# Counts of edges beside the keys, and x + b0 a step earlier, in a graph layer kernel

## The chip, the cores and the metric

The kernel runs on one core of one Trainium2 chip. The metric is the device time of one execution in microseconds (us). Before the change three runs took 4014.95, 4014.03 and 4009.7 us, median 4014.03. A core has five engines that the text speaks of by their names or by those of the profile: TensorE (PE, its weight loads PEld), VectorE (DVE), ScalarE (ACT), GpSimd (POOL) and SyncE (SP), which starts the transfers. Each works through its own instructions in order, and waits for the others by semaphores.

## The reference

There are 32 independent graphs of 512 nodes with 128 features. About one entry in 16 of an adjacency matrix is not zero.

```
# layer 0: normalised graph convolution, added to x, layernorm
adj1 = adj + I;  dinv = adj1.sum(axis=2) ** -0.5
x = layernorm(x + dinv[:,:,None] * adj1 * dinv[:,None,:] @ (x @ weight) + bias)
# layer 1: a message for every pair of nodes, weighted by adj, summed
m_j = x @ W1[:D];  m_i = x @ W1[D:]
msg = gelu(layernorm(m_j[:, None] + m_i[:, :, None] + b1, g1, be1))   # pair (i, j)
agg = einsum('bijo,bij->bio', msg, adj)
x = layernorm(x + layernorm(concat([x, agg]) @ W2 + b2, g2, be2))
```

## The kernel before, in words

A message is needed only where adj is not zero, so the kernel lists the neighbours of every node and works through lists. For a batch (one graph) it makes `key`, which is the variance term of the message at edges and 0 elsewhere; VectorE's top-8 operations find the edges from it in slots of eight (`lists`), then up to 16 more (`more`), which are shared out over two further slots (`shared`). A batch is 41 groups: 8 slots of 4 groups, one group of own edges, and 2 slots of 4.

A group runs through a pipeline, one group behind the other (`pairs`, `sums`, `weights`, `messages`, `aggregate`): TensorE gathers the features of the neighbours by matmuls with one-hot matrices into one of three PSUM buffers `u` (L724, L725); VectorE adds to it and leaves `u_sb` (L734), which frees the buffer; GpSimd multiplies adjacency values with the one-hot matrix, the weight product `sw` (L749, four buffers); ScalarE makes four Gelus `m` (L763); TensorE sums with `agg` (L772). At the end of a batch ScalarE copies agg (L781), and `finish` does the last layernorms of that batch during the next one: on VectorE the statistics (L194, L196), on GpSimd rstd and shift (L199 to L205) and three products (L645, L647, L649), on ScalarE the scaling (L208).

Beside the groups of one batch the kernel prepares the next ones. Each preparation is a Python generator that is advanced a few steps per group; a table `plan` says in which groups: `layer0` of the next batch has 26 steps over the first 22 groups of the current batch, `more` and `shared` of the current batch run from group -10 to 28. For ScalarE, GpSimd and VectorE the instructions stand in the order in which the program writes them in this loop; TensorE and SyncE are ordered by a planner. What comes before the loop, batch 0's preparation among it, is ordered by the planner on all engines.

The steps of `layer0` that matter here, in order: transposes of the adjacency into `a_t`, and on ScalarE a pass over each quarter that sums the degrees (`copied`, L260); on VectorE `mask`, -1 at edges and 0 elsewhere, in bf16 (L263); two pauses; on GpSimd the degree chain deg1, none, degp, rdeg, dinv, dinv2 (L277 to L287) and `xb` = x + b0 (L289); on ScalarE four passes over the mask that count the edges (L293), then `s` and `own_s`, the features scaled by dinv (L297, L302), from the PSUM tile psup; two steps later GpSimd adds own_s to xb (L306) and TensorE makes `pconv` in two halves of eight matmuls (L311); VectorE makes y (L318), its statistics follow, GpSimd's rstd and shift, ScalarE's x1 (L208), TensorE's transposes (L220), and so on to the keys: in five steps (L358) TensorE makes pv (L365) and VectorE reads it a step later, twice for each quarter (L361, L362). The counts of edges are read by GpSimd much later, in `shared` (L499), to see that no edge was missed.

`shared` runs at the same time as these last steps, with the shared slots of the current batch: L469 to L479 on VectorE right after `more` ends; then 16 pairs of matmuls `pl` on TensorE (L537), each copied by ScalarE into `sent` (L533), and `chosen` on VectorE (L553), which reads all of `sent` and lies in the same buffer as the mask. The PSUM tiles outside the pipeline come from a pool of four banks.

Of the kernel before, what the change touches and what calls it, by code (L numbers as in the profile page):

```python
# [8 lines left out]
F32 = mybir.dt.float32  # L9
BF16 = mybir.dt.bfloat16  # L10
I32 = mybir.dt.int32
U32 = mybir.dt.uint32
AF = mybir.ActivationFunctionType
ALU = mybir.AluOpType
# [4 lines left out]
P = 128  # L19
# [8 lines left out]
def bcast(ap, n):  # L28

    return ap.unsqueeze(1).to_broadcast([ap.shape[0], n, ap.shape[-1]])  # L30
# [16 lines left out]
def sparse_path(ctx, tc, x, adj, w0, b0, w1, b1, g1, be1, w2, b2, g2, be2, out, most):  # L47
# [21 lines left out]
    nc = tc.nc  # L69
    B, N, D = x.shape  # L70
    C = N // P
# [3 lines left out]
    node = ctx.enter_context(tc.tile_pool(name="node", bufs=1))  # L75
    small = ctx.enter_context(tc.tile_pool(name="small", bufs=2))
# [66 lines left out]
    rows = {}  # L143
# [69 lines left out]
    def bank(key):  # L213
        return ps.tile([P, 512], F32, tag="ps", name=key)
# [10 lines left out]
    def pause(n):  # L225

        for _ in range(n):
            yield

    def layer0(b):  # L230

        st = state[b] = {}
        xs = node.tile([P, C, D], F32, tag="xs", name=f"xs_{b}")
# [7 lines left out]
        edges = small.tile([P, C], F32, tag="edges", name=f"edges_{b}")  # L241
        st["edges"] = edges
        deg = small.tile([P, C], F32, tag="deg", name=f"deg_{b}")
        mask = big.tile([P, C, N], BF16, tag="mask", name=f"mask_{b}")
        px = transposed(xs, f"x_{b}")
        for mc in range(C):
# [12 lines left out]
            copied = small.tile([P, N], BF16, tag="copied", name=f"copied_{b}_{mc}", bufs=1)  # L259
# [11 lines left out]
            if mc == 0:  # L271
                x_t = node.tile([P, N], F32, tag="t0", name=f"x_t_{b}")
                nc.scalar.copy(x_t, px)
        yield from pause(2)

        deg1 = small.tile([P, C], F32, tag="deg1", name=f"deg1_{b}")
        nc.gpsimd.tensor_scalar(deg1, deg, 1.0, None, ALU.add)  # L277
# [7 lines left out]
        nc.gpsimd.tensor_sub(dinv, rdeg, none)  # L285
        dinv2 = small.tile([P, C], F32, tag="dinv2", name=f"dinv2_{b}", bufs=1)
        nc.gpsimd.tensor_tensor(dinv2, dinv, dinv, ALU.mult)  # L287
        xb = node.tile([P, C, D], F32, tag="t2", name=f"xb_{b}")
        nc.gpsimd.tensor_tensor(xb, xs, bcast(rows["b0"], C), ALU.add)  # L289

        for q in range(C):
            copied = small.tile([P, N], BF16, tag="copied", name=f"counted_{b}_{q}", bufs=1)
            nc.scalar.activation(copied, mask[:, q, :], AF.Copy, accum_out=edges[:, q : q + 1])  # L293

        s = node.tile([P, C, D], F32, tag="t1", name=f"s_{b}")
        for c in range(C):
# [60 lines left out]
        key = big.tile([P, C, N], F32, tag="key", name=f"key_{b}")  # L357
        for q in range(C + 1):  # L358
            if q:
                here = key[:, q - 1, :]  # L360
                nc.vector.scalar_tensor_tensor(here, pt, a_sum[:, q - 1 : q], c_sum, ALU.add, ALU.add)  # L361
                nc.vector.scalar_tensor_tensor(here, here, -TINY, mask[:, q - 1, :], ALU.min, ALU.mult)  # L362
            if q < C:
                pt = bank(f"pv_{b}_{q}")
                nc.tensor.matmul(pt, at2[:, q * P : (q + 1) * P], ct, start=True, stop=True)  # L365
            yield
# [417 lines left out]
    def advance(gens, steps=1):  # L784
# [13 lines left out]
    n_groups = len(order)  # L798
    plan = [
        (layer0, 26, -n_groups, -19),  # L800
        (lists, 21, -19, -8),
        (parts, 7, -19, -10),
# [343 lines left out]
```

## Time and profile before

| | |
|---|---|
| runs, median (lowest to highest) | 4014.03 us (4009.7 to 4014.95) |
| the profiled execution's own time | 4011.64 us |
| its span, first to last instruction | 4009.9 us |
| mean granted TensorE clock | 0.985 |
| TensorE matmuls / weight loads busy | 3766.3 us (94%) / 3510.3 us (88%) |
| VectorE, ScalarE, GpSimd busy | 3263.9 us (81%), 2791.9 us (70%), 2225.5 us (55%) |
| the four counts of a batch (L293), passes alone | 128 passes, 80.1 us, mean 626 ns |
| xb (L289) | 32 times, 40.7 us, mean 1273 ns |
| the mask (L263) | 32 times, 39.0 us, mean 1218 ns |
| s / own_s (L297, L302) | 128 each, 361 ns / 394 ns |

The profile records one execution, instruction by instruction. A row of the timeline has the start in us from the first instruction, the duration, the engine, the line of the program, the operation, what it writes and reads, and how many alike follow each other (x4); in brackets the idle time of the engine ahead of it, and what ended it. A row of the list of waits has the waiting instruction, what it waited for, the time in total, how often, and the longest. A row of a table by stretches has the stretch, its length, the busy time of the five engines with the number of instructions, the granted clock (1.00 is full), the share of the DMA engines and GB/s. Busy time alone says little: an engine that works all the time may only be the one that all wait behind, and a wait matters only where nothing later takes its place.

### The profile page before, as it was taken

How to read it: one execution, taken by the hardware profiler on the slowest of the kernel's cores; microseconds unless marked ns; L12 is line 12 of the kernel's file. 1: busy time of each engine (PE TensorE's matmuls, PEld its weight loads, DVE VectorE, ACT ScalarE, POOL GpSimd, SP SyncE). 2: the span in 40 equal slices, each digit the busy share in tenths (PEclk: the TensorE clock that was granted, in tenths of full speed). 3: DMA queues.
4: the chain of work that ended last, by engine and by line, in shares of the span. 5: the costliest groups of instructions: out<-in, count | busy, mean ns of one | idle time of the engine just before them, and what ended most of it. 6: DMA issues, size and time to landing. Idle time of an engine off the chain costs nothing. (4 is left out here: it accounts for less than half of the span.)

```text
span 4009.9 us, 108439 instructions
## 1 busy us (share of the span) xinstructions
PE 3766.3 (94%) x39744; PEld 3510.3 (88%) x39744; DVE 3263.9 (81%) x10645; ACT 2791.9 (70%) x8321; POOL 2225.5 (55%) x2526
## 2 busy tenths in 40 slices
PE   5999999999999999999999999999999999999997
PEld 5988889888899888898888998888998889888887
DVE  6888888888887888888888888888888888788892
ACT  4777677676776766776767767667767677676664
POOL 4555565555655555655556555556555565555554
PEclk7999999999999999999999999999999999999998
DMA  3444444444444444444444444444444444444442
GB/s 85 107 109 106 114 101 106 107 107 105 113 102 106 108 106 110 106 106 106 107 105 113 102 106 108 106 112 104 106 105 108 105 108 106 108 107 105 98 105 56
DMA packets 902107, 419.99 MB, mean 105 GB/s; under 512 B 724304, under 2 KB 882192, under 8 KB 901568
## 3 DMA queue, kind: packets, MB, share of 16 engines
q1 hardware_dynamic: 901344, 412.52, 44.1%
q8 instruction: 317, 5.19, 0.5%
q14 instruction: 222, 1.82, 0.1%
q0 software_dynamic: 224, 0.46, 0.1%
HBM read 227.15 MB, written 13.76 MB: 60 GB/s over the span
## 5 line engine op out<-in xcount | busy, mean ns | idle before, releaser
L749 POOL TENSOR_TENSOR sw<-mt,a_t 128x512 f32<-128x512 bf16 x1056 | 1216.8, 1164 | 918.1 <-PE agg L772 764.0
L772 PE MATMUL agg<-sw,m 128*128 128x128 f32 x10496 | 1495.7, 285 | 76.2 <-POOL sw L749 46.1
L724 PE MATMUL u<-c,s 128*128 128x128 bf16 x15744 | 1433.9, 220 | 84.0 <-DVE u_sb L734 80.3
L763 ACT ACTIVATE m<-u_sb,r 128x128 f32<-128x128 f32 x4096 | 1294.0, 395 | 142.3 <-DVE u_sb L734 57.8
L772 PEld LDWEIGHTS agg<-sw,m 128*128 128x128 f32 x10496 | 1304.5, 192 | 94.2 <-POOL sw L749 51.3
L724 PEld LDWEIGHTS <-s 128*128 128x128 bf16 x15744 | 1191.2, 98 | 115.0 <-issue 40.9
L725 PE MATMUL u<-be,sd_rows 128*128 128x128 bf16 x5248 | 1148.6, 220 | 20.7 <-DMA sd_rows<-sd_ds 14.6
L734 DVE TENSOR_TENSOR u_sb<-u,ac 128x512 f32<-128x512 f32 x1056 | 713.4, 676 | 200.6 <-PE u L725 177.1
L725 PEld LDWEIGHTS <-sd_rows 128*128 128x128 bf16 x5248 | 512.7, 98 | 30.7 <-issue 20.0
L763 ACT ACTIVATE m<-u,r_s 128x128 f32<-128x128 f32 x1024 | 288.3, 363 | 251.6 <-PE agg L772 247.4
L533 ACT COPY sent<-pl 128x352 f32<-128x352 f32 x512 | 228.9, 447 | 315.9 <-PE pl L537 278.8
L687 DVE TENSOR_SCALAR s<-raw,node_p 128x2052 bf16<-128x2052 bf16 (+1 forms) x352 | 421.5, 1197 | 20.6 <-DMA raw<-idx_ds 11.9
L720 PE MATMUL u<-ac,sj 128*128 128x128 f32 x2048 | 437.8, 296 | 0.0
L749 POOL TENSOR_TENSOR sw<-mt,sent 128x512 f32<-128x512 bf16 x256 | 296.4, 1163 | 229.0 <-PE agg L772 176.2
L537 PEld LDWEIGHTS pl<-a_t,sj 128*128 128x128 f32 x2048 | 316.2, 191 | 60.7 <-issue 59.2
L457 DVE MAX8 a_t<-key 128x8 f32<-128x128 f32 x1024 | 301.2, 294 | 34.5
L537 PE MATMUL pl<-a_t,sj 128*128 128x176 f32 x2048 | 327.4, 313 | 1.3 <-POOL a_t L505 1.3
L522 DVE TENSOR_SCALAR sj<-pj,node_p 128x512 f32<-128x512 f32 x256 | 187.7, 745 | 153.8 <-PE pj L526 153.8
L720 PEld LDWEIGHTS u<-ac,sj 128*128 128x128 f32 x2048 | 310.0, 192 | 0.4
L458 DVE FIND_INDEX8 idx_m<-a_t,key 128x8 uint32<-128x128 f32 x1024 | 291.4, 285 | 0.0
L311 PEld LDWEIGHTS pconv<-s,a_t 128*128 128x128 f32 x1024 | 141.3, 214 | 57.1 <-ACT s L297 55.4
L361 DVE SCALAR_TENSOR_TENSOR key<-pv,a_sum,c_sum 128x512 f32<-128x512 f32 x128 | 95.7, 748 | 108.3 <-PE pv L365 108.3
(178 smaller groups left out, 4788.8 us busy)
## 6 DMA issues: line engine op xcount, KB each, us to landing
raw<-idx_d SPq DMA_DIRECT2D x256, 513.0 KB
raw<-idx_ds SPq DMA_DIRECT2D x64, 513.0 KB
a_nat<-in_adj_dram SPq DMA_DIRECT2D x32, 1024.0 KB
sd_rows<-sd_d SPq DMA_DIRECT2D x768, 12.0 KB
xs<-in_x_dram SPq DMA_DIRECT2D x32, 256.0 KB
out_dram<-o_sb SPq DMA_DIRECT2D x32, 256.0 KB
mt<-s SPq DMA_TRANSPOSE x352
raw<-idx_ds SPq DMA_DIRECT2D x32, 129.0 KB
```

What stands on the lines that cost most here:

```text
L457: nc.vector.max(found, k)
L458: nc.vector.max_index(idx[:, n, h : h + 8], found, k)
L533: nc.scalar.copy(sent[:, n - 1], pt[:, : SHARED * WIDE].rearrange("p (k w) -> p k w", w=WIDE))
L537: nc.tensor.matmul(pt[:, k * WIDE : (k + 1) * WIDE], sj[:, n, k * P : (k + 1) * P], at[:, n, :], start=True, stop=True,)
L687: nc.vector.tensor_scalar(s.rearrange("p (k e) -> p k e", k=3), raw, node_p, None, ALU.is_equal)
L720: nc.tensor.matmul(pu[:, c, :], place, state[b]["ac"][:, q, 0, :], start=first, stop=False)
L724: nc.tensor.matmul(pu[:, c, :], here, c3[:, k, c, :], start=(first and k == 0), stop=False)
L725: nc.tensor.matmul(pu[:, c, :], dev[:, q, c, :], be9, start=False, stop=(c == C - 1))
L734: nc.vector.tensor_tensor(u, pu, a if t == EXTRA else bcast(a[:, q, :], C), ALU.add)
L749: nc.gpsimd.tensor_tensor(sw, mt[:, 0] if t == EXTRA else mt[:, :, q, :], a, ALU.mult)
L763: nc.scalar.activation(m[:, c, :], u[:, c, :], AF.Gelu, scale=r[:, k : k + 1])
L772: nc.tensor.matmul(st["agg"][:, c, :], m[:, c, :], sw[:, c, :], start=(begin and c == 0), stop=(end and c == C - 1),)
```

## The change

Three edits in `layer0`. `xb` is made in the second of the two paused steps, so one step ahead of the degree chain, instead of behind it. The four counting passes are taken out of the step that makes `s`. Each of them is put into one of the four steps of the keys in which VectorE reads a quarter, ahead of that reading.

```
@@ layer0
-        yield from pause(2)
+        yield
+        xb = node.tile([P, C, D], F32, tag="t2", name=f"xb_{b}")
+        nc.gpsimd.tensor_tensor(xb, xs, bcast(rows["b0"], C), ALU.add)
+        yield
 
         deg1 = small.tile([P, C], F32, tag="deg1", name=f"deg1_{b}")
         nc.gpsimd.tensor_scalar(deg1, deg, 1.0, None, ALU.add)
@@
         nc.gpsimd.tensor_tensor(dinv2, dinv, dinv, ALU.mult)
-        xb = node.tile([P, C, D], F32, tag="t2", name=f"xb_{b}")
-        nc.gpsimd.tensor_tensor(xb, xs, bcast(rows["b0"], C), ALU.add)
-
-        for q in range(C):
-            copied = small.tile([P, N], BF16, tag="copied", name=f"counted_{b}_{q}", bufs=1)
-            nc.scalar.activation(copied, mask[:, q, :], AF.Copy, accum_out=edges[:, q : q + 1])
 
         s = node.tile([P, C, D], F32, tag="t1", name=f"s_{b}")
@@ the keys
         for q in range(C + 1):
             if q:
+
+                copied = small.tile([P, N], BF16, tag="copied", name=f"counted_{b}_{q}", bufs=1)
+                nc.scalar.activation(copied, mask[:, q - 1, :], AF.Copy, accum_out=edges[:, q - 1 : q])
                 here = key[:, q - 1, :]
                 nc.vector.scalar_tensor_tensor(here, pt, a_sum[:, q - 1 : q], c_sum, ALU.add, ALU.add)
```

In the changed program's order of instructions, VectorE and SyncE are as before. On GpSimd each xb stands seven places earlier: behind the shift of the layernorm in `finish` (L205), ahead of one weight product and of deg1. On ScalarE the four counts stand, in the loop, each behind the Gelus of one of the groups that carry `sent` copies: behind the first copy and before the second, before the sixth, before the twelfth, and before the last. In batch 0 they stand where they stood. On TensorE only the place of pconv's first half changes: it stood among the matmuls of the u of slot 2's second group, and the agg behind it was spread among them too; now two of its matmuls, two of the agg, one, two and five follow each other ahead of that u.

## The prediction

> **What bounds the kernel now.** I read the page's busy shares first, then the list of waits, then the timeline of one batch, and last the same stretch in all batches.
>
> ```profile
> PE 3766.3 (94%) x39744; PEld 3510.3 (88%) x39744; DVE 3263.9 (81%) x10645; ACT 2791.9 (70%) x8321; POOL 2225.5 (55%) x2526
> ```
> ```profile
> PE u L724 <- DVE u_sb L734: 80.3, 69, 2.2
> PEld pconv L311 <- ACT s L297: 55.4, 31, 6.7
> PE agg L772 <- POOL sw L749: 46.1, 30, 1.6
> PE agg L772 <- ACT m L763: 30.0, 20, 1.5
> ```
>
> TensorE is busy for 94%, but its few gaps lie at fixed places of each batch. The second wait line is the one that the change seems made for: once a batch pconv waits for `s`, which stands behind ScalarE's four counts. Whether that gap is worth anything depends on what ends later. I take the batch whose copy of agg (L781) starts at 1907.70; its period is 122.21 us. The timeline of all engines, columns start and duration in us:
>
> ```profile
> 1916.51 1.17 POOL L749 TENSOR_TENSOR sw<-mt,a_t 128x512 f32<-128x512 bf16 x1
> ...
> 1917.64 0.23 POOL L277 TENSOR_SCALAR deg<-deg 128x4 f32<-128x4 f32 x1
> ...
> 1918.14 1.22 DVE L263 TENSOR_SCALAR mask<-a_t 128x2048 bf16<-128x2048 f32 x1
> ...
> 1918.27 1.15 POOL L281 TENSOR_TENSOR degp<-deg,none 128x4 f32<-128x4 f32 x1
> ...
> 1920.98 0.61 ACT L293 ACTIVATE counted<-mask 128x512 bf16<-128x512 bf16 x1
> ...
> 1921.05 1.27 POOL L289 TENSOR_TENSOR xb<-xs,b_row 128x512 f32<-128x512 f32 x1
> ```
> ```profile
> 1925.75 1.27 POOL L647 TENSOR_TENSOR un<-un,be_row 128x512 f32<-128x512 f32 x1
> ...
> 1925.96 1.33 DVE L469 SCALAR_TENSOR_TENSOR over<-a_t,sharing 128x256 f32<-128x256 f32 x1
> ...
> 1926.98 1.45 POOL L306 TENSOR_TENSOR xb<-xb,own_s 128x512 f32<-128x512 f32 x1
> ```
> ```profile
> 1943.69 1.16 PE L772 MATMUL agg<-sw,m 128*128 128x128 f32 x8 [1.54 <-POOL sw L749]
> ```
>
> GpSimd works without a gap from 1914.59 to 1931.9, VectorE from 1910.2 on. VectorE reaches y (L318) at 1933.01 without having waited, its mean and variance go to GpSimd at 1935.25, GpSimd is again without a gap until the four weight products at 1942.47, and TensorE stands 1.54 us for the first of them. So in this third of the batch the chain GpSimd and VectorE, layernorm, GpSimd sets the time, not TensorE. The program shows it twice over, since some batches run the first half of pconv at half the clock. Two batches, 559.77 and 2029.91, TensorE's timeline, and their window of four us each (PEclk is the third number from the end):
>
> ```profile
> 581.50 1.95 PE L311 MATMUL pconv<-s,a_t 128*128 128x128 f32 x16
> ...
> 591.41 1.27 PE L772 MATMUL agg<-sw,m 128*128 128x128 f32 x8 [1.52 <-ACT m L763]
> ```
> ```profile
> 2053.27 1.95 PE L311 MATMUL pconv<-s,a_t 128*128 128x128 f32 x16
> ...
> 2061.60 1.27 PE L772 MATMUL agg<-sw,m 128*128 128x128 f32 x8
> ```
> ```profile
> 576.60:580.60 4.00, 3.99 (x41) 3.91 (x40) 3.89 (x8) 4.00 (x16) 4.00 (x5) 1.00 0.10 28
> ...
> 2046.70:2050.70 4.00, 3.96 (x22) 3.82 (x22) 3.90 (x8) 4.00 (x15) 4.00 (x5) 0.57 0.06 18
> ```
>
> Counted from each batch's copy, TensorE begins the second half of pconv at 21.73 in one and at 23.36 in the other, 1.63 us apart; y stands at 25.33 and 25.34 and that agg at 31.64 and 31.69. TensorE being 1.63 us earlier bought nothing.
>
> **The change part by part**, per batch, 31 batches in the loop.
>
> Counts out of the step of `s`: 4 x 0.75 us from start to start leave ScalarE; the first stood at 1920.98, `s` at 1923.86. Now `s` waits for dinv only. With xb in front, GpSimd ends dinv at about 1922.02 (below), so `s` comes some 1.8 us earlier. The new order on TensorE also places pconv's first half, with the agg of one group between, ahead of the whole next u instead of among it. This closes part of the 1.50 us gap that TensorE has before 1924.52 (that row names u_sb, ending at 1924.47; pconv's load waited 1.62 until then). Kept to the end: 1.50 x 31 = 46 us. By the two batches above, kept: 0; the time reappears at 1939.33 and 1943.69.
>
> Counts beside the keys: each stands behind a group's four Gelus and ahead of the `sent` copies. A copy that follows such a pass starts 0.61 to 0.63 after it. Three of the four meet a wait of ScalarE for pl of 1.93 us (1960.91, 1966.00, 1972.28) and vanish. The fourth does not:
>
> ```profile
> 1973.82 1.28 ACT L763 ACTIVATE m<-u_sb,r 128x128 f32<-128x128 f32 x4
> 1975.00 0.43 ACT L533 COPY sent<-pl 128x352 f32<-128x352 f32 x1
> ...
> 1976.24 1.23 DVE L553 SCALAR_TENSOR_TENSOR chosen<-sent,place_k 128x256 f32<-128x256 f32 x1
> ```
>
> That last copy moves to 1975.62 and ends at 1976.05. `chosen` reads all of `sent`, and its buffer is the mask's, so it also waits for the fourth count, a new wait, over by 1975.81. VectorE gets there at 1976.24: 0.19 us to spare, 0. Behind `chosen` VectorE is busy up to the indices for idx_h, for which TensorE waits in most batches, so without that cover it is 0.62 x 31 = 19 us. The Gelus behind move 0.62; their agg is 1.8 us after the first of them. The banks of the moved copies are wanted over 0.6 us later.
>
> xb: GpSimd's order puts it seven places up, ahead of one weight product and the degrees. 1.23 from start to start leave one place and enter another: 0 on GpSimd's own sum. The weight product moved back is read by TensorE after 1924: hidden. But the mask now meets something else. In the trace the mask holds up degp (1.15 instead of its shortest 0.20), and L469 cannot start before L647 (1.33 instead of 0.43). The Trainium skill, page "SBUF — State Buffer", section "Who interferes with whom", has the rule: a VectorE operation in a two-port mode, or with two SBUF inputs, and a GpSimd operation exclude each other for a whole instruction, first come first served. That speaks against this change: the weight product will run 1917.74 to 1918.91, and the mask, due at 1918.14, meets it. A blocked operation here ends as if begun 0.16 before the GpSimd end (L469: 1927.29 - 0.43 = 1926.86 against 1927.02), so the mask runs 1918.75 to 1919.97, 0.61 late. By the rule alone that is 0.61 x 31 = 19 us on VectorE. By the row it is 0: VectorE comes 0.61 later to L469, at 1926.57, and that waits for L647 until 1926.83 in any case. And GpSimd: deg1 ends 0.06 after the mask (as degp did), 1920.03; none, degp and rdeg start 0.08, 0.39 and 0.67 later; dinv is done at 1922.02, the next weight product starts at 1922.25 against 1922.28. It loses to the mask what it lost before. I take 0, bounds -0.1 and +0.1 a batch, 3 us either way.
>
> Half clock: it follows gaps of 0.84 and 1.50 us within 3.4 us. The page "TensorE: Matmul & The Clock Gate", part 1, halves the clock after an idle window of about 3.4 us; here 2.34 us of gaps were enough, so the row decides. After the change I count 1.45 (the next u waits for u_sb, 0.61 later) and 0.4 for the Gelus before the agg: 1.85. By the page, no half clock: 1.4 us saved in the one batch where y waited (0.92, at 2914) and 0.05 in ten others, -2 us. If it stays in 11 batches, y comes 0.3 late: +3. I take -1.
>
> Start: the first batch is ordered outside the written order; there the counts still stand ahead of `s`. 0.
>
> Sum: 0 + 0 + 0 - 1 = -1 on the profiled execution's 4011.64, of which the span is 4009.9; the runs' median is 2.4 above it. So about 4013.
>
> **The rivals.**
> TensorE keeps its gap: 4014 - 46 = 3968. For it: pconv <- s 55.4 us. Against: the two batches.
> The lock costs GpSimd less: were the mask not held by the weight product, degp's lost 0.95 would shrink and rdeg start 0.64 earlier; 0.64 x 31 = 20, 3994. Against: L479 (0.83 for four elements) ends with the weight product beside it.
> Slower by the lock: L469 has 0.26 us of room. If VectorE is later than about 0.87, L306 takes the ports first and L469, with the layernorm behind it, waits 1.23 more: 38 us, 4052. For it: only that margin.
> Slower by the fourth count: 0.2 to 0.62 a batch if `chosen` is ready sooner or ScalarE later: 4020 to 4033.
>
> **How the numbers follow.** Absorbed 0.66 (own range 4007 to 4020); gap kept 0.08; lock cheaper 0.08; lock lost 0.08; fourth count shows 0.10. 0.2% is 8 us, about what the runs can tell from no change. Faster 0.16, same 0.66, slower 0.18. The range leaves out the gap kept and the lock lost: 3993 to 4033.
>
> **What would show it.** `s` near 14.4 us after the copy of agg instead of 16.16; the mask at 1.8 us instead of 1.22, degp at 0.20; L469 still ending near 19.6; y near 25.3; the wait of agg for sw still about 1.5 or more; `chosen` at 68.5. It is wrong if y or `chosen` moves by more than 0.3 us in most batches.

## The result, and the profile after

| kernel | median | lowest to highest | runs |
|---|---|---|---|
| before, on the same chip | 4012.14 us | 4008.56 to 4016.68 | 12 |
| after | 4012.22 us | 4007.93 to 4016.84 | 12 |

The ratio is 0.9998, with a 95% interval of 0.9991 to 1.0006: no difference that can be measured. The forecast was 4013. The profiled execution of after took 4011.93 us, its mean granted clock is 0.985, as before. Its page:

```profile
span 4010.2 us, 108407 instructions
...
PE 3759.7 (94%) x39744; PEld 3502.1 (87%) x39744; DVE 3262.1 (81%) x10645; ACT 2785.8 (69%) x8321; POOL 2226.4 (56%) x2526
```

The total hides that the inside of a batch did change. The waits of after (us in total, times, longest):

```profile
ACT sent L533 <- PE pl L537: 221.4, 126, 3.1
...
PE agg L772 <- ACT m L763: 64.3, 31, 2.1
...
PE u L724 <- DVE u_sb L734: 54.5, 40, 2.2
...
ACT s L294 <- POOL dinv L288: 32.5, 31, 1.3
...
PE agg L772 <- POOL sw L749: 27.7, 22, 1.5
```

The wait of pconv for `s`, 55.4 us before, is gone from the list, and ScalarE now waits for dinv instead. TensorE's wait for u_sb fell by 25.8 us (from 80.3), and its wait for the Gelus `m` rose by 34.3 (from 30.0). That is the picture of time that moves, not of time that is gained. ScalarE's wait for pl fell by 57.4 us: the counts now lie in it.

The same batch as in the prediction, in after's timeline; its copy of agg starts at 1909.96:

```profile
1920.01 1.17 POOL L749 TENSOR_TENSOR sw<-mt,a_t 128x512 f32<-128x512 bf16 x1
...
1920.41 1.85 DVE L263 TENSOR_SCALAR mask<-a_t 128x2048 bf16<-128x2048 f32 x1
...
1921.14 1.20 POOL L280 TENSOR_SCALAR deg<-deg 128x4 f32<-128x4 f32 x1
...
1922.74 0.20 POOL L284 TENSOR_TENSOR degp<-deg,none 128x4 f32<-128x4 f32 x1
...
1924.37 1.14 ACT L294 ACTIVATE s<-psup,dinv 128x128 f32<-128x128 f32 x4 [1.03 <-POOL dinv L288]
...
1928.04 1.27 POOL L647 TENSOR_TENSOR un<-un,be_row 128x512 f32<-128x512 f32 x1
...
1928.86 0.74 DVE L469 SCALAR_TENSOR_TENSOR over<-a_t,sharing 128x256 f32<-128x256 f32 x1
...
1929.27 1.45 POOL L303 TENSOR_TENSOR xb<-xb,own_s 128x512 f32<-128x512 f32 x1
...
1935.31 1.08 DVE L315 SCALAR_TENSOR_TENSOR y<-pconv,dinv,xb 128x128 f32<-128x128 f32 x4
```

The mask is held by the weight product (1.85 us instead of 1.22), it holds up deg1 (1.20 instead of 0.23), and degp no longer loses anything (0.20 instead of 1.15). `s` starts 14.41 us after the copy instead of 16.16. L469 starts 0.6 us later than before and still ends at 19.64 (19.59 before), because it had waited for L647 before and now hardly does. y stands at 25.35 against 25.31. Over the 30 full batches the median of y moved from 25.33 to 25.37, that of `chosen` from 68.55 to 68.59.

### The profile page after: what moved, and what is told of

The parts are those of the page before. It is cut to its first block, busy times and chain, and to the rows that moved or that the text cites. A ratio compares the mean times of both kernels' runs of the same rounds, so it can differ in the third digit from the quotient of the medians.

```text
span 4010.2 us, 108407 instructions
## 1 busy us (share of the span) xinstructions
PE 3759.7 (94%) x39744; PEld 3502.1 (87%) x39744; DVE 3262.1 (81%) x10645; ACT 2785.8 (69%) x8321; POOL 2226.4 (56%) x2526
## 5 line engine op out<-in xcount | busy, mean ns | idle before, releaser
L724 PE MATMUL u<-c,s 128*128 128x128 bf16 x15744 | 1411.5, 220 | 58.1 <-DVE u_sb L734 54.5
L522 DVE TENSOR_SCALAR sj<-pj,node_p 128x512 f32<-128x512 f32 x256 | 187.6, 745 | 156.4 <-PE pj L526 156.4
L400 DVE FIND_INDEX8 idx<-top,key 128x8 uint32<-128x128 f32 x512 | 145.7, 285 | 0.0
```

The costliest lines, as they stand in the source:

```text
L724: nc.tensor.matmul(pu[:, c, :], here, c3[:, k, c, :], start=(first and k == 0), stop=False)
```

## The experiments

Each was timed in turn with the kernel before on one chip, not the same chip for all; the median of before was 4013.51 us for e1 to e4, 4013.46 for e5 to e8, 4016.32 for e9 to e11 and 4011.0 for e12, so the ratios are what to compare.

| label | median, us | ratio to before | 95% interval |
|---|---|---|---|
| e1_counts_alone | 4020.12 | 1.0016 | 1.0010 to 1.0023 |
| e2_xb_alone | 4022.88 | 1.0027 | 1.0017 to 1.0038 |
| e3_no_counts | 4010.66 | 0.9995 | 0.9987 to 1.0003 |
| e4_counts_twice | 4022.91 | 1.0027 | 1.0018 to 1.0036 |
| e5_fourth_twice | 3992.09 | 0.9946 | 0.9933 to 0.9960 |
| e6_dve_late_a | 4011.85 | 0.9998 | 0.9990 to 1.0007 |
| e7_dve_late_b | 4054.22 | 1.0104 | 1.0088 to 1.0119 |
| e8_after_checks_late | 3978.35 | 0.9910 | 0.9895 to 0.9925 |
| e9_before_checks_late | 3991.68 | 0.9944 | 0.9931 to 0.9958 |
| e10_shift_64 | 3992.87 | 0.9943 | 0.9930 to 0.9957 |
| e11_late_aligned | 3959.17 | 0.9857 | 0.9842 to 0.9872 |
| e12_counts_twice_in_place | 4046.46 | 1.0090 | 1.0073 to 1.0107 |

### Each half alone

e1 does the first half alone:

```
@@ layer0, ahead of s
-        for q in range(C):
-            copied = small.tile(...)
-            nc.scalar.activation(copied, mask[:, q, :], AF.Copy, accum_out=edges[:, q : q + 1])
@@ the keys
             if q:
+                copied = small.tile(...)
+                nc.scalar.activation(copied, mask[:, q - 1, :], AF.Copy, accum_out=edges[:, q - 1 : q])
```

> The kernel before, with ScalarE's four counts of edges moved beside the keys, and x + b0 left where it was. My theory (the chain of GpSimd and VectorE through dinv, the first step of the shared stage and the layernorm sets the first 36 us of a batch, so that ScalarE's counts are off the path): within 4 us of the kernel before, 4008 to 4016; s begins near 14.4 us after the aggregation's copy instead of 16.2, y stays at 25.3. The rival that TensorE's gap of 1.50 us behind s is worth its length: 3966 to 3985. If the fourth count were on the way to the selection: 4020 to 4033.

Measured: 4020.12, 6.6 us slower than before (4013.51). `s` begins at 13.3 us, not at 14.4 (with `xb` left behind it, dinv is done at 13.12), and y stays at 25.34, so the gap is worth nothing, as my theory has it, but the time is outside of what it allowed. The cause is further on. TensorE's rows of e1 in the batch whose copy starts at 3017.34, and stretches of 4 us of e1 and then of after in the batch of the same number (columns: length, busy time of PE, PEld, DVE, ACT, POOL, granted clock, DMA share, GB/s):

```profile
3045.44 0.33 PE L723 MATMUL u<-c,s 128*128 128x128 bf16 x3 [0.54 <-DVE u_sb L733]
...
3048.98 2.05 PE L771 MATMUL agg<-sw,m 128*128 128x128 f32 x8 [2.48 <-ACT m L762]
```
```profile
3045.34:3049.34 4.00, 1.41 (x18) 1.27 (x18) 3.97 (x18) 2.44 (x8) 3.67 (x6) 0.85 0.20 73
3049.34:3053.34 4.00, 4.00 (x25) 3.66 (x25) 4.00 (x9) 3.65 (x12) 3.59 (x10) 0.50 0.41 78
3053.34:3057.34 4.00, 4.00 (x39) 3.75 (x37) 1.75 (x4) 2.53 (x9) 4.00 (x4) 0.80 0.99 236
```
```profile
3041.49:3045.49 4.00, 1.89 (x26) 1.73 (x25) 3.96 (x17) 2.39 (x7) 3.67 (x6) 1.00 0.33 120
3045.49:3049.49 4.00, 2.51 (x29) 2.20 (x27) 4.00 (x9) 3.65 (x12) 3.59 (x10) 1.00 0.40 75
```

What TensorE no longer waits at 16 us it waits at 28 to 32 us, in one piece, and behind that longer wait the clock is halved. In the trace's record of the clock, one episode at half clock lasts 3.41 us, which is 1.7 us of clock lost, and a double one 6.83 us. In e1 there is one near 31 us in 21 of the 30 batches, a double one in 8 of these, and those 8 are just the ones in which `chosen` comes 0.8 to 1.1 us later than in the same batch of before. The 30 periods add up to 3685.5 us, before to 3679.0. The 8 batches with a double episode are 7.3 us longer than in before, and the other 22 together 0.8 shorter: that is the difference.

e2 does the second half alone: `xb` a step earlier, the counts left ahead of `s`.

```
-        yield from pause(2)
+        yield
+        xb = node.tile(...); nc.gpsimd.tensor_tensor(xb, xs, bcast(rows["b0"], C), ALU.add)
+        yield
@@
-        xb = node.tile(...); nc.gpsimd.tensor_tensor(xb, xs, bcast(rows["b0"], C), ALU.add)
```

> The kernel before, with x + b0 alone made a step earlier, and the counts left ahead of s. My theory (the mask ends 0.6 us later beside x + b0, and the wait for the scatter's table takes that up): 4008 to 4018, mask near 1.87 us long, y at 25.3 to 25.4. If each of the 31 batches paid the 0.6 us: about 4031. If taking x + b0 out of the chain behind dinv were worth its 0.4 to 0.6 us: about 3995 to 4000.

Measured: 4022.88, 9.4 us slower and outside of my range. In 21 of 30 batches y stands at 25.4, so the mask's 0.6 us is absorbed as expected. The other nine cost it all. The two pconv halves and y of e2 in a batch of each kind (copies at 929.26 and 1051.39), and 4 us of each around the first half:

```profile
947.67 1.33 PE L311 MATMUL pconv<-s,a_t 128*128 128x128 f32 x10
951.62 1.95 PE L311 MATMUL pconv<-s,a_t 128*128 128x128 f32 x16
954.62 1.09 DVE L318 SCALAR_TENSOR_TENSOR y<-pconv,dinv,xb 128x128 f32<-128x128 f32 x4
```
```profile
1070.62 2.45 PE L311 MATMUL pconv<-s,a_t 128*128 128x128 f32 x10
1076.58 1.95 PE L311 MATMUL pconv<-s,a_t 128*128 128x128 f32 x16
1078.57 1.13 DVE L318 SCALAR_TENSOR_TENSOR y<-pconv,dinv,xb 128x128 f32<-128x128 f32 x4 [0.92 <-PE po L487]
```
```profile
945.80:949.80 4.00, 3.07 (x29) 3.01 (x29) 3.90 (x12) 4.00 (x16) 4.00 (x4) 1.00 0.20 61
1067.90:1071.90 4.00, 3.04 (x15) 2.92 (x15) 3.90 (x12) 4.00 (x16) 4.00 (x4) 0.51 0.20 64
```

u_sb comes 0.6 us later behind the late mask, and pconv with it: its second half ends at 24.31 instead of 23.67 us after the copy. At full clock that is still ahead of y. With a half-clock episode in the first half it ends at 25.9 (five batches, y 0.6 late) or, with a double one, near 27.1 (four batches, y 1.7 to 1.9 late). Summed over these nine, y is 10.2 us late; in before it is late in one batch, by 1.4. The 30 periods are 9.4 us longer than before's.

So neither half is free alone, and together they are. The traces show why. The early `s` takes pconv away from y (its end is 23.13 us in after, in every batch), so the late mask can no longer hurt there; and dinv, which the early `xb` puts at 14.39 instead of 13.12, keeps `s` and pconv from being as early as in e1, so the wait near 31 us is 2.1 us instead of 2.5 with another 0.54 ahead of it, and double episodes are 1 in 30 instead of 8.

### ScalarE's counts

e3 leaves the counts of edges out of the changed kernel.

```
-                copied = small.tile(...)
-                nc.scalar.activation(copied, mask[:, q - 1, :], AF.Copy, accum_out=edges[:, q - 1 : q])
@@ shared
-        nc.gpsimd.tensor_tensor(missed, missed, st["edges"], ALU.add)
+        nc.gpsimd.tensor_tensor(missed, missed, missed, ALU.subtract)
```

> The changed kernel with ScalarE's four counts of edges a batch left out altogether, so that the number of missed edges is not computed (GpSimd's three small instructions on it stay). It takes 4 x 0.69 us of ScalarE work from each batch, about 86 us in all. My theory (ScalarE's counts lie wholly beside other work): 4006 to 4013, the time of the changed kernel, with ScalarE's waits longer by what is left out. If ScalarE were what sets the end of a batch: down to 3930. If only the fourth count is in the way of the selection: some 0.2 us a batch or less, 4005.

Measured: 4010.66, ratio 0.9995: 86 us of ScalarE's work are worth nothing in their new place. `chosen` begins at 68.60. Without the tile of counts all tiles behind it begin 64 bytes earlier in SBUF. The next section shows that such a shift can matter; here the transposing transfers take 1.8 to 1.9 us as in after, so it hides no price.

e5 puts a second pass ahead of the fourth count.

```
             if q:
+                if q == C:
+                    edges2 = small.tile([P, 1], F32, tag="edges2", name=f"edges2_{b}")
+                    copied = small.tile(...)
+                    nc.scalar.activation(copied, mask[:, q - 1, :], AF.Copy, accum_out=edges2)
                 copied = small.tile(...)
                 nc.scalar.activation(copied, mask[:, q - 1, :], AF.Copy, accum_out=edges[:, q - 1 : q])
```

> The changed kernel with a second pass of 0.63 us ahead of the fourth count, so that the last copy into sent ends some 0.7 us later. This prices the margin of 0.2 us between that copy's end (68.39 us after the aggregation's copy) and the first chosen key (68.59). My theory: chosen begins 0.5 us later, near 69.1, and the selection behind it is the path, so 31 x 0.5 = 15 us: 4020 to 4032. If the selection had room behind it, or the copies ahead of it gave way: 4008 to 4016.

Measured: 3992.09, 21 us faster than before, which none of my theories had. Two things happen. The first is at `chosen`, in after and then in e5:

```profile
1733.35 0.43 ACT L533 COPY sent<-pl 128x352 f32<-128x352 f32 x1
1733.75 1.16 POOL L749 TENSOR_TENSOR sw<-mt,a_t 128x512 f32<-128x512 bf16 x1 [3.92 <-PE agg L772]
1733.97 1.62 DVE L553 SCALAR_TENSOR_TENSOR chosen<-sent,place_k 128x256 f32<-128x256 f32 x2
```
```profile
1724.38 1.17 POOL L753 TENSOR_TENSOR sw<-mt,a_t 128x512 f32<-128x512 bf16 x1 [3.92 <-PE agg L776]
...
1724.73 0.43 ACT L537 COPY sent<-pl 128x352 f32<-128x352 f32 x1
1725.20 1.02 DVE L557 SCALAR_TENSOR_TENSOR chosen<-sent,place_k 128x256 f32<-128x256 f32 x2 [0.52 <-ACT sent L537]
```

In after `chosen` starts at 68.59 us from the copy, but its two instructions take 1.62 us, since a weight product of GpSimd began 0.22 us before and holds the ports. In e5 it starts at 69.19, when most of that product is over, takes 1.02, and both end at 70.21. The copy ends 0.75 us later than in after, and that costs `chosen` nothing: the room is not 0.2 us but at least 0.75. That makes this pass free; it doesn't make it a gain. The gain is the second thing, and the two kernels e4 and e5 have it in common.

### What made e5 faster

e4 is the kernel before with the counts made twice ahead of `s`.

```
+        edges2 = small.tile([P, C], F32, tag="edges2", name=f"edges2_{b}")
+        for q in range(C):
+            copied = small.tile(...)
+            nc.scalar.activation(copied, mask[:, q, :], AF.Copy, accum_out=edges2[:, q : q + 1])
         for q in range(C):
```

> The kernel before with the four counts made twice ahead of s, so that s begins about 2.8 us later (near 19 us behind the aggregation's copy). This prices the place that the change clears. My theory: between the end of pconv and y there are 1.6 us of room where TensorE runs at its full clock and about none where it runs at half, so y comes 1 to 2.5 us later in a batch, and the time is 4037 to 4090. If ScalarE were the path in this place (2.8 us in each of 31 batches, both ways): about 4099. If s is as far from the path as its earlier start is: 4012.

Measured: 4022.91, less than my theory's range. `s` begins at 19.2 us, y at 26.15 to 26.45, so 0.8 to 1.1 us later, some 27 us over the batches; only 9.4 arrived. In e4 and e5 alone, every second transposing transfer is issued in 1.6 us instead of 1.8 to 1.9, and a wait of TensorE near 104.5 us of each batch is gone. What they share beside more ScalarE work is the tile `edges2`, by which all that lies behind that pool in SBUF begins 64 bytes later. e10 is after with this shift alone and not one instruction more:

```
-        edges = small.tile([P, C], F32, tag="edges", name=f"edges_{b}")
+        edges = small.tile([P, 4 * C], F32, tag="edges", name=f"edges_{b}")[:, :C]
```

> The changed kernel with the small tile of edge counts allocated four times as wide and not used beyond its first four columns: no instruction differs, and all that lies behind that pool in SBUF (the one-hot rows s, the scatter matrices mt, the pair buffers) begins 64 bytes later. In the two kernels that had 64 bytes more there (the counts made twice, the fourth count made twice) every second transposing DMA was issued in 1.6 us instead of 1.8 to 2.0, and TensorE's wait of 0.3 us for the rows of deviations near 104.5 us was gone; of the two buffers of s one then starts at a multiple of 256 bytes (189,696), and in the other kernels neither does. If the place in SBUF is what made the kernel with the fourth count twice faster: 3988 to 3996, every second transpose at 1.6 us. If it was ScalarE's longer stream or the later selection: 4008 to 4016.

Measured: 3992.87, ratio 0.9943, as e5 (0.9946). SyncE's timeline of after and of e10 at the same place of the batch, TensorE's row of after behind it (e10 has no such wait in 25 of its 30 batches, after none without one), and all transfers in the first us from the transpose's first packets in each, 1766.42 to 1767.42 in after and 1759.20 to 1760.20 in e10:

```profile
1765.24 1.76 SPq L689 DMA_TRANSPOSE mt<-s  x1
1767.05 0.97 SPq L705 DMA_DIRECT2D sd_rows<-sd_ds  x1
```
```profile
1758.04 1.57 SPq L689 DMA_TRANSPOSE mt<-s  x1
1759.65 0.45 SPq L705 DMA_DIRECT2D sd_rows<-sd_ds  x1
```
```profile
1769.97 0.22 PE L725 MATMUL u<-be,sd_rows 128*128 128x128 bf16 x1 [0.32 <-DMA sd_rows<-sd_ds]
```
```profile
DMA packets 784, 0.20 MB, mean 201 GB/s; under 512 B 784, under 2 KB 784, under 8 KB 784
```
```profile
DMA packets 1042, 0.27 MB, mean 267 GB/s; under 512 B 1042, under 2 KB 1042, under 8 KB 1042
```

The rows of deviations stand behind the transpose in SyncE's queue: they are issued by 102.64 us after the copy of agg in after and by 101.85 in e10, and TensorE's wait for them goes. In the medians over the batches, TensorE's sums with agg run 0.2 us earlier in e10 from 91 us on, and 0.7 us earlier from 106 us on. So this wait is some 0.5 us of the 0.7 that a batch gains; the 0.2 us near 90 us were not followed up.

e12 takes the shift out of e4: the same second passes, but written into `edges` itself, so that nothing moves in SBUF.

```
+        for q in range(C):
+            copied = small.tile(...)
+            nc.scalar.activation(copied, mask[:, q, :], AF.Copy, accum_out=edges[:, q : q + 1])
         for q in range(C):
```

> The kernel with the four counts made twice ahead of s, once more, but with both passes writing the same tile, so that nothing in SBUF moves. If the 64 bytes hid 22 us of the price there: 4038 to 4050, with waits of 0.2 to 0.3 us near 105 us back, every transpose again at 1.8 to 2.0 us, and y 0.8 to 1.1 us later than in the kernel before as it was there. If three more microseconds ahead of s really cost only the 9 us of that run: 4018 to 4028.

Measured: 4046.46, ratio 1.0090, with `s` at 19.2 and y at 26.15 to 26.5 as in e4. The place in SBUF had hidden 26 us of a price of 35. The profiled execution, the shortest of e12's four, is 30.9 us longer than before's: 27.9 in the 30 batches, most of it at y, and 4.9 ahead of the first copy of agg, less 2.0 in the last batch. The mechanism is not the one that I had written down for e4, room between pconv and y. It is GpSimd, in e12's batch with its copy at 1681.05:

```profile
1702.47 1.28 POOL L309 TENSOR_TENSOR xb<-xb,own_s 128x512 f32<-128x512 f32 x1 [2.09 <-ACT own_s L305]
...
1706.13 0.87 DVE L194 BATCH_NORM_STATS2 stats_l<-un 128x6 f32<-128x128 f32 x4 [0.71 <-POOL un L652]
...
1707.20 1.09 DVE L321 SCALAR_TENSOR_TENSOR y<-pconv,dinv,xb 128x128 f32<-128x128 f32 x4
```

Behind the late `s` comes a late own_s, GpSimd waits for it, its product for the layernorm is late, and VectorE waits for that ahead of y. So `s` may be earlier at no gain, but 3 us later costs 35 us. The counts' old place was at no cost only because it ended early enough.

### The ports at L469

e6 and e7 give VectorE one more reduction right behind the mask in the changed kernel.

```
+                idle = small.tile([P, 1], F32, tag="idle", name=f"idle_{b}", bufs=1)
+                nc.vector.tensor_reduce(idle, a_nat[:, 0, :128], AX.X, ALU.add)
```

> The changed kernel with one more reduction over 128 elements on VectorE right behind the mask, about 0.2 us, whose result nobody reads. My theory: VectorE reaches the shared stage's first product (18.91 us) some 0.2 us later, still before GpSimd's product with own_s can take the ports near 19.3, so that product still ends before 20 us and y stays within 0.2 us of 25.37: 4008 to 4018. If the room is already used up: 4040 or more.

Measured: 4011.85, y at 25.37: free. e7 is the same with `:512`.

> As the one before, with 512 elements, about 0.6 us. My theory: VectorE now comes after GpSimd has taken the ports at 19.3, so the product waits until about 20.6 us, and y comes 1.0 to 1.3 us later: 31 x 1.0 to 1.3, 4035 to 4055. If there is no such race for the ports and VectorE is simply 0.6 us later: at most 4031. If VectorE has room here anyway: 4008 to 4016.

Measured: 4054.22, y at 26.59, 1.22 us later. In e7's timeline, where `over` is L471 and the copy stands at 1679.79:

```profile
1697.88 1.28 POOL L649 TENSOR_TENSOR un<-un,be_row 128x512 f32<-128x512 f32 x1
1699.11 1.27 POOL L305 TENSOR_TENSOR xb<-xb,own_s 128x512 f32<-128x512 f32 x1
1699.29 1.38 DVE L471 SCALAR_TENSOR_TENSOR over<-a_t,sharing 128x256 f32<-128x256 f32 x1
```

GpSimd's sum starts 0.18 us ahead of VectorE's product, and the product ends at 20.88 instead of 19.65: 0.4 us more of lateness on VectorE than in e6, where it came at 19.10, turns into 1.2 us, 41 us over the kernel. The changed kernel reaches this point at 18.9.

### A shorter chain ahead of y

If VectorE's chain sets y, work taken out of it must pay. e8 is the changed kernel with four small instructions of the first step of `shared` (two comparisons and two sums) moved to just before their result is read; e9 is the kernel before with the same move.

```
-        nc.vector.tensor_scalar(here, st["top"], 0.0, None, ALU.is_gt)
-        nc.vector.tensor_reduce(counts[:, 0, :], here..., AX.X, ALU.add)
-        nc.vector.tensor_scalar(counts[:, 1, :], var[:, own, 0], 0.0, None, ALU.is_gt)
...
-        nc.vector.tensor_reduce(counts[:, 2, :], count..., AX.X, ALU.add)
...
+        nc.vector.tensor_scalar(here, st["top"], 0.0, None, ALU.is_gt)
+        nc.vector.tensor_reduce(counts[:, 0, :], here..., AX.X, ALU.add)
+        nc.vector.tensor_scalar(counts[:, 1, :], var[:, own, 0], 0.0, None, ALU.is_gt)
+        nc.vector.tensor_reduce(counts[:, 2, :], count..., AX.X, ALU.add)
         nc.vector.tensor_reduce(missed, counts.rearrange("p k q -> p q k"), AX.X, ALU.add)
```

> The changed kernel with four small reductions of VectorE (the counts for the check of missed edges) moved from the first step of the shared stage to just before the result is used, so that VectorE's chain ahead of y is 1.5 to 1.9 us shorter. pconv ends at 23.13 us in every batch of the changed kernel and y begins at 25.37, so up to 1.9 us are to be had in a batch. My theory (that chain, and not TensorE or ScalarE, sets y): y at 23.6 to 24.6 us, 3955 to 3990. If the layernorm's GpSimd steps or the ports set y whatever VectorE does: 4005 to 4015. Half clock behind longer waits of TensorE could take 10 us back.

> The kernel before with VectorE's four small reductions moved just ahead of the use of their result, the same move that took the changed kernel from 4012 to 3978. It tells whether the given change is worth something once VectorE's chain ahead of y is shorter. My theory: here pconv ends at 23.7 us at full clock and at 25.3 at half clock, so y can begin near 24.3 where the clock is full and waits for pconv where it is half, in about a third of the batches: 3978 to 3995. If pconv were ahead of y in every batch: 3974 to 3982, no different from the changed kernel with the same move. If the earlier s is needed in every batch: 4005 or more.

Measured: e8 3978.35, e9 3991.68. In e8 y begins at 24.25 in every batch, 1.12 us earlier; it doesn't get all 1.9, since the statistics ahead of it now wait 0.68 us for GpSimd's product `un`. 31 times 1.12 is 35 us, what e8 gained. In e9 y begins at 24.2 in 21 batches and at 25.3 in the nine in which a half-clock episode delays pconv, as in this one (copy at 2752.21):

```profile
2775.56 1.95 PE L311 MATMUL pconv<-s,a_t 128*128 128x128 f32 x16
2777.55 1.13 DVE L318 SCALAR_TENSOR_TENSOR y<-pconv,dinv,xb 128x128 f32<-128x128 f32 x4 [0.92 <-PE po L479]
```

(The row names `po`, which stands right behind pconv on TensorE.) So the change is worth something once the chain that hid it is shorter: e8 and e9 differ by 0.34% in their ratios to before, whose intervals don't meet, some 13 us.

e11 adds to e8 that both buffers of the one-hot rows `s` of the groups, and `mt`, start at multiples of 256 bytes:

```
-        edges = small.tile([P, C], F32, tag="edges", ...)
+        edges = small.tile([P, 4 * C], F32, tag="edges", ...)[:, :C]
-        missed = small.tile([P, C], F32, tag="missed", ...)
+        missed = small.tile([P, 4 * C], F32, tag="missed", ...)[:, :C]
@@ gathers
-        s = onehot.tile([P, n * N + PAD], BF16, ...)
+        wide = n * N + PAD if t == EXTRA else (n * N + PAD + P - 1) // P * P
+        s = onehot.tile([P, wide], BF16, ...)[:, : n * N + PAD]
```

> The changed kernel with VectorE's four small reductions late (3978 by itself), and with both buffers of the one-hot rows s, and the scatter matrices mt, at multiples of 256 bytes (the buffers of s widened to 4352 bytes, 96 bytes more ahead of them). If the transposing DMA reads faster from a start at a multiple of 256 bytes: all transposes near 1.6 us where no large load runs beside them, and at least the 20 us of the shift by 64 bytes on top of 3978, so 3935 to 3960. If only one of the two buffers is ever on the path: 3955 to 3960. If the start is not what counts: 3974 to 3982.

Measured: 3959.17, 1.4% faster than before, the fastest of all. The median batch takes 120.69 us, against 121.42 in e8 and 122.52 in after. Against e8 the ratio fell by 0.53%; one aligned buffer brought 0.55% in e10. So the second buffer and `mt` brought nothing that shows.

## Why the prediction was right, and where its steps were not

**Counts out of the step of `s`: kept 0.** Right. `s` came 1.74 us earlier (1.8 forecast), and y did not move. The time reappears where it was said to: the wait of agg at 31.66 us after the copy is 2.10 us now, and that at 36.02 still 1.54 in the 17 batches without half clock. The rival that TensorE keeps its gap (3968) is out: the counts moved alone made the kernel slower.

**Counts beside the keys: 0.** Right by the time and by e3. But the step "0.19 us to spare, and without that cover 19 us" was mis-sized: I read the start of `chosen` as the deadline, and its two instructions show by their length that the first one is held by GpSimd. e5, against e10 with the same place in SBUF, gives the room as at least 0.75 us. The rival of the fourth count (4020 to 4033) rested on the same misreading.

**`xb` and the lock: 0, bounds 0.1 a batch.** Right. Mask, deg1 and degp changed as worked out, dinv was done at 14.38 (14.32 forecast), the next weight product started at 14.61 (14.55), and L469 ended at 19.65. The rule of the Trainium skill, page "SBUF — State Buffer", section "Who interferes with whom", holds in these rows, and its price of 19 us did not come, because the next lock wait on VectorE took it up. What the working missed is that this absorption holds for VectorE's path only. TensorE's u_sb is on VectorE too, and by it pconv came 0.6 us later; alone that costs 9.4 us (e2). In the full change the earlier `s` covers it, which I had not seen as a condition. The rival "lock cheaper" is out: degp's lost 0.95 us turned up again in deg1.

**The margin at L469.** The rival "slower by the lock" (4052) is a true mechanism with nearly the price given: e7 took 4054. The room was forecast as 0.26 us; 0.2 us more are free, 0.6 us too many. The change stays on the safe side.

**Half clock: -1.** The size is right to within what the runs can tell, but that is luck, for the working is not right. I let the episodes at 16 us go or stay. They went, all of them, and came back behind the wait near 31 us, in 13 of 30 batches. I had named that wait as the place where the time reappears, and did not ask what it does to the clock. The one batch where y had waited (1.4 us) was won, and one with a double episode, in which `chosen` came 1.9 us late, was lost. By the page "TensorE: Matmul & The Clock Gate", part 1, an idle window of about 3.4 us is needed; here waits of 2.1 us in one piece were enough in these 13 batches, and in the other 17 the same wait had no such effect. Nor are "gaps of 0.84 and 1.50 us within 3.4 us" enough, as the working had it: before has both in all 30 batches, and an episode in 11. What the traces show in its place is that a fixed grid of 3.41 us decides, by how much of the wait falls into one of its stretches (last section).

**Start: 0.** The first copy of agg stands at 190.17 us instead of 190.53.

## What to carry to other kernels

A wait that the profile lists by its total is worth nothing until one knows what ends later in the same stretch: here two batches of one trace, one with TensorE 1.6 us later than the other and the same y, told it before any run. Parts of a change are not additive: each half of this one costs 7 to 9 us alone, and the other half takes away what causes it. And an experiment that adds a tile also moves every tile behind it, so make a control that moves them without the work, or keep the new work in a tile that is already there.

## What the runs showed of the hardware that I had not expected

**The start of the source of a transposing transfer.** The two buffers of `s` lie at 185,504 and 189,632 bytes in before and after, as the compiled programs place them. The transposes (SyncE's rows: lowest, median and highest ns of issuing one) in after, e10 and e11:

```profile
L689 SPq DMA_TRANSPOSE mt<-s x352: 1189/1893/5662, 62.5 to 3963.0; - x176
```
```profile
L689 SPq DMA_TRANSPOSE mt<-s x352: 1195/1801/6377, 65.5 to 3949.7; - x176
```
```profile
L690 SPq DMA_TRANSPOSE mt<-s x352: 1195/1618/6278, 65.6 to 3910.6; - x176
```

In e4, e5 and e10 one buffer starts at 189,696, a multiple of 256, and only every second transpose is at 1.6 us; in e11 both do, and all are (where no large load runs beside them). In e6 and e7 (32 bytes further than after) and e3 (64 bytes back) neither does, and nearly all stay at 1.7 to 2.0; e3's second buffer is at a multiple of 128, so that isn't enough. The page "DMA: Bandwidth & Descriptors" of the Trainium skill, section "DMA Transpose (X-bar)", asks for 32 bytes; all kernels here have that, and 256 bytes bought 20 us and more. The packets of these transfers are of about 256 bytes (0.27 MB in 1042), which would fit. That it is the start of the source is read from the pattern over these kernels; why packets from another start are slower is open. In e11 the buffers `mt` were aligned as well, so a share of theirs is not excluded there; in e10 they are not.

**A fixed grid decides whether a wait brings half clock.** In each of the 14 traces the changes of the granted clock lie whole multiples of 3.413 us apart, to 0.001 us over the whole execution, although the batches' lengths vary from 120.3 to 125.3 us. So I added up TensorE's idle time in each stretch of that grid. Here is the stretch with the longest part of the wait near 31 us, and the one behind it, in two batches of after (copies at 803.67 and 1909.96; columns as above):

```profile
831.83:835.24 3.41, 1.40 (x21) 1.22 (x19) 3.38 (x15) 1.98 (x6) 3.08 (x6) 1.00 0.31 112
835.24:838.65 3.41, 3.31 (x15) 3.00 (x16) 3.41 (x10) 3.06 (x10) 3.00 (x9) 0.50 0.13 25
```
```profile
1937.74:1941.15 3.41, 1.78 (x24) 1.59 (x23) 3.38 (x14) 1.61 (x5) 2.99 (x7) 1.00 0.33 120
1941.15:1944.56 3.41, 2.82 (x29) 2.55 (x29) 3.41 (x10) 3.06 (x11) 3.00 (x8) 1.00 0.04 9
```

The wait is 2.1 us long in both. In the first batch 2.0 us of it fall into one stretch, TensorE is idle for 2.0 of 3.41 us, and the next stretch is at half clock. In the second batch the grid cuts the wait into 1.6 and 0.5 us, and the clock stays. Over the 14 traces, between the first copy of agg and the last but one: behind a full-clock stretch with over 1.93 us idle came half clock in all 162 cases, with up to 1.75 us in none of 14,621, and in between in 28 of 70. A half-clock stretch was followed by another in all 17 cases with over 0.58 us idle, and in none with under 0.48; that makes the double episodes. This is read from the traces alone; no run moved the grid.

So the sum of the waits says little. TensorE's three waits for u_sb, m and sw add up to 146.5 us in after and 156.4 in before, and the clock lost over the span is 60.0 us in after and 58.2 in before. In e1 it is 87.3: there the wait for m is 2.48 us, with another of 0.54 close ahead of it, so over 1.93 us of idle time fall into one stretch more often.

**Order at the ports, not their load.** The change added two lock waits, 0.6 us on the mask and 1.0 us on deg1, and neither moved y; in e7 one instruction that came 0.18 us after GpSimd's cost 1.2 us in each batch.
